# A norm's mean from chunk sums on POOL or DVE and one matmul with ones, in a Mamba and feed-forward layer on one Trainium2 core

## The chip, the core and the metric

The kernel runs on one core of a Trainium2 chip. The metric is the device time of one execution in microseconds (us); lower is better. The engines are named as in the profile: PE (TensorE, matmuls), PEld (its weight loads), DVE (VectorE), ACT (ScalarE), POOL (GpSimd) and SP (SyncE, which here issues nearly all DMAs). All data are fp32.

## The reference

The input x has 8 sequences of 384 channels and 32 x 32 = 1,024 positions. What is computed, cut to what matters:

```python
def ln(v, eps):                       # over the 384 channels of a position
    m = v.mean(channels); s = v.var(channels)
    return (v - m) / sqrt(s + eps)

# for each sequence
t  = ln(ln(x, 1e-6), 1e-5) * ln_w + ln_b
xm, z = split(t @ in_proj.T)          # 768 + 768
xc = silu(conv3(xm) + conv_b)         # causal, along the positions
dt, Bm, Cm = split(xc @ x_proj.T)     # 24, 16, 16
dt = softplus(dt @ dt_proj.T + dt_b)  # 768
h  = exp(dt * A) * h + dt * xc * Bm   # recurrence along positions: 768 x 16 states
y  = ((h * Cm).sum(states) + xc * D) * silu(z)
t  = gelu((y @ out_proj.T) @ w1.T + b1) @ w2.T + b2
x  = x + t
# for the first 5 sequences: binarised weights, absmax quantisation per sequence
t  = quant(gelu(quant(ln(x, 1e-5) @ W1b.T + b1)) @ W2b.T + b2)
x  = x + t                            # sequences 5 to 7: quant returns zeros, so x stays
```

## The kernel before

**Tiles.** Channels lie on the 128 partitions in KC = 3 chunks, positions along the free axis in two halves of T = 512 columns. A tile of 384 channels and one half is [128, 3, 512]. Weights come in 128 x 128 blocks as the stationary operand.

**Stages.** `s1` makes the two norms (as one, with a joint eps), the input projection (p_in, p_z), the convolution, dt, B and C for each half of a sequence and stores them in HBM. `s2` with `scan` and `scan_pair` is the recurrence: 12 units to a sequence, in each four groups of four states; per group POOL multiplies by B (line 968), ACT makes the exponentials (line 577, tile da, in PSUM), DVE scans (line 993), POOL or DVE multiplies by C, and PE sums the states of two groups with eight matmuls of 32 columns (line 933, py). The first and the last sequence are scanned in two halves, the others whole. `s3` is the output projection and the MLP (p_out, p_h, p_o). `ffn` is the feed-forward part of the first five sequences (p_y). `binarise` prepares its weights once.

**The norm.** `norm` (line 610) is called 26 times: 16 times from `s1`, 10 times from `ffn`. For the mean, `columns` sums over the channels with matmuls against ones. There are twelve of them (line 619, p_sum), each 128 x 32 against 128 columns. Three accumulate for each of four column groups, which lie in the four 32-partition strips of the array. The result is scaled by -1/384 on ACT or DVE (tile mean), and `spread` (line 637, p_mean) brings it to all partitions by four matmuls with a broadcast column of the identity. DVE adds it to the three chunks (line 649). The variance goes the same way: ACT squares (tile sq), twelve matmuls (p_var), a scaling, a small matmul that turns it (line 659), an add, a power on POOL (line 665), `spread` again (p_r) and a multiplication on DVE (line 669).

**The order.** Nothing is left to a scheduler at run time. `Plan` is a planner in the kernel's own code: each operation is added with an engine, a cost in us, what it reads and writes, and perhaps a second engine with another cost (`others`). `Plan.run` walks through time in a model, takes for each engine the operation that `choose` and `rank` prefer among those that are ready, and emits it; so each engine's queue gets its order. Costs are constants and small functions (MM for a whole 128x512 matmul, `c_act`, `c_dve`, `c_pair`, `c_pool`), `LAG` is what an engine may overlap, SIGNAL and DRAIN what a hand-over costs, `land` and `size` stand for a DMA. TURNS holds a number for each 100 us of the model's time; it turns the order of operations of equal rank and has bits that let scans or stages go first. On DVE and POOL an operation outside the scan is preferred to the scan's own unless a bit says otherwise. Where the model sees PE idle for more than IDLE = 0.7 us, it emits small matmuls that nobody reads (line 471, spare) so that PE goes on working.

**Rings.** Every tile is taken from a ring of a fixed number of buffers (lines 428 to 445), and an operation that needs a new tile waits for a free one. The rings named below are front (7 buffers, results of `s1`), w_f (3, its weights), dt_r (3, dt for the scan), sq (1, squares and the product dt * xc) and mm (3, PSUM for matmuls).

Of the kernel before, what the change touches and what calls it, by code (L numbers as in the profile page):

```python
# [70 lines left out]

MM = 0.86
SWITCH = 0.22
# [18 lines left out]
TURNS = (  # L92
    17610, 24087, 20212, 39788, 55575, 59023, 81989, 22321, 58617, 812894,
    311620, 51673, 560357, 59520, 80314, 2104, 50573, 559844, 6159, 58063,
    51278, 41401, 6390, 863060, 0, 672911, 34250, 39179, 27191, 131575,
)
# [7 lines left out]

LAG = {"ACT": 0.09, "DVE": 0.08}

# [9 lines left out]
def c_pair(n):  # L116
    return 0.22 + n * 0.00188

# [78 lines left out]
class Op:  # L197
    __slots__ = (
        "engine", "cost", "emit", "prio", "slack", "table", "size",
        "wants", "next", "ready", "tiles", "others", "settle", "land",  # L200
    )


class Plan:
# [12 lines left out]
    def add(self, engine, cost, emit, r=(), w=(), claim=(), table=None, size=0, others=None,  # L217
            land=1.6, rate=350e3):
        op = Op()
        op.engine, op.cost, op.emit, op.table = engine, cost, emit, table  # L220
        op.others, op.settle = others or {}, None
        op.size, op.land, op.prio = 0.03 + size / rate, land + 0.2, (*self.prio, len(self.ops))
        op.next, op.ready, op.tiles = [], 0.0, []
        op.slack = SLACK if self.prio[0] < 0 else 0.0
        deps = set()

        def parts_of(t):
            t, part = t if isinstance(t, tuple) else (t, None)
            if t not in op.tiles:
                op.tiles.append(t)  # L230
                if t.ring is not None:
                    t.left += 1
            if part is None:
                if None not in t.parts:
                    t.parts[None] = [None, []]
                return list(t.parts.values())
            if part not in t.parts:
                whole = t.parts.get(None)
                t.parts[part] = [whole[0], list(whole[1])] if whole else [None, []]
            return [t.parts[part]]  # L240

        for t in claim:
            t.left += 1
            op.tiles.append(t)
        for t in r:
            for p in parts_of(t):
                if p[0] is not None:
                    deps.add(p[0])
                p[1].append(op)
        for t in w:  # L250
            for p in parts_of(t):
                if p[0] is not None:
                    deps.add(p[0])
                deps.update(p[1])
                p[0], p[1] = op, []
        deps.discard(op)
        op.wants = len(deps)
        for d in deps:
            d.next.append(op)
        self.ops.append(op)  # L260
        return op

    def run(self):
# [5 lines left out]
        free["PE"] = 2 * SIGNAL  # L269
        table, dma_free, clock = None, 0.0, Clock()  # L270
        left, scanned = len(self.ops), 0
# [17 lines left out]
        def choose(e, now, able):  # L289
            able = [op for s, op in able if s <= now]  # L290
            at = int(now / STRETCH)
            turn = TURNS[at] if at < len(TURNS) else 0
            if e == "ACT":
                same = [op for op in able if op.table == table and table != "exp"]
                plain = [op for op in able if op.table in (None, "exp")]
                able = same if table is not None and same else plain or able
                if turn & ACT_STAGES:
                    able = [op for op in able if op.prio[0] > 0 and op.table in (None, "exp")] or able
                if len(self.spare.ring.free) <= SCARCE:
                    able = [op for op in able if self.spare.ring in map(ring_of, op.tiles) and (  # L300
                        op.table in (None, "exp", table))] or able
            if e in ("DVE", "POOL"):

                scans = [op for op in able if op.prio[0] == 0]
                if not (turn & (DVE_SCANS if e == "DVE" else POOL_SCANS) and scans):
                    able = [op for op in able if (
                        op.prio[0] > 0 and op.ready <= now - PATIENCE)] or scans or able
                else:
                    able = scans
            return min(able, key=lambda op: rank(op, turn))  # L310
# [29 lines left out]
        while left:  # L340
# [28 lines left out]
            if e == "PE":  # L369
                while now - free[e] > IDLE and self.spare.ring.free[0:] and (  # L370
# [7 lines left out]
                    free[e] = clock.run(free[e], MM / 2)  # L378
                    heapq.heappush(ring.free, free[e])
            for t in taken_by(op):  # L380
                heapq.heappop(t.ring.free)
                t.ring.taken[t.lane] += 1
                t.real = t.ring.make(t.shape, t.name)
            op.emit()
            cost = op.cost
            if op.table is not None and op.table != table:
                cost += LOAD_TABLE
                table = op.table
            end = clock.run(now, cost) if e == "PE" else now + cost
            free[e] = end - LAG.get(e, 0.0)  # L390
            if e == "SP":
# [19 lines left out]
class Layer:  # L411
    def __init__(self, ctx, tc, a, out):
# [9 lines left out]
        def ring(tag, bufs, where=sbuf):  # L422
# [6 lines left out]

            "front": ring("front", 7), "t_f": ring("t_f", 2), "w_f": ring("w_f", 3),  # L430
            "dbc": ring("dbc", 1), "halo": ring("halo", 2),

            "dt_r": ring("dt_r", 3), "dtx_r": ring("dtx_r", 2), "u": ring("u", 3),
            "xr": ring("xr", 1), "zr": ring("zr", 1), "state": ring("state", 1),
# [7 lines left out]

            "mm": ring("mm", 3, psum), "sq": ring("sq", 1),
            "rstd": ring("rstd", 2), "root": ring("root", 2),
# [127 lines left out]

    def act(self, out, in_, func, cost, r, w, table=None, **kw):

# [4 lines left out]
            }),  # L579
            r=r, w=w, table=table,  # L580
        )

    def affine(self, out, in_, r, w, bias=0.0, scale=1.0, n=T, pool=False):
# [21 lines left out]
        else:  # L605
            others = {"DVE": (c_dve(n) + (0 if isinstance(scale, float) else 0.15), on(nc.vector))}
        extra = 0.0 if plain else 0.09 if isinstance(scale, float) else 0.18
        self.plan.add("ACT", 0.16 + n * 0.00083 + extra, on_act, r=r, w=w, others=others)

    def norm(self, t, eps, scale):  # L610

        nc, add = self.nc, self.plan.add
        def columns(src, name):
# [10 lines left out]

            add("PE", 0.78, emit, r=[src], w=[p])
            return p

        def spread(src, name, turned=False):
# [12 lines left out]

            add("PE", 0.98, emit, r=[src], w=[p])
            return p

        p_sum = columns(t, "p_sum")
        mean = self.piece("rstd", [P, TG], "mean")
        self.affine(lambda: mean.real, lambda: p_sum.real, [p_sum], [mean], scale=-1.0 / C, n=TG)
        p_mean = spread(mean, "p_mean")
        add("DVE", c_dve(KC * T), lambda: nc.vector.tensor_add(
            t.real, t.real, p_mean.real.unsqueeze(1).to_broadcast([P, KC, T])  # L650
        ), r=[p_mean], w=[t])
# [6 lines left out]
        p_turned = self.piece("mm", [P, G], "p_turned")  # L658
        add("PE", 0.3, lambda: nc.tensor.matmul(
            p_turned.real, var.real, self.ident[:, ::DQ], start=True, stop=True  # L660
        ), r=[var], w=[p_turned])
        rstd = self.piece("root", [P, G], "rstd")
        add("DVE", 0.1, lambda: nc.vector.tensor_scalar_add(rstd.real, p_turned.real, eps),
            r=[p_turned], w=[rstd])
# [10 lines left out]
    def s1(self, b):  # L675
# [45 lines left out]
        for half, cols in enumerate(HALVES):  # L721
# [58 lines left out]

            add("PE", 0.15 + KC * MM, low, r=[w, *all_m], w=[p_dbc], claim=[dbc])
            self.affine(lambda dbc=dbc: dbc.real, lambda p_dbc=p_dbc: p_dbc.real, [p_dbc], [dbc])
# [12 lines left out]
            for k in range(0, KD, 2):  # L795
# [14 lines left out]

                add("PE", MM + 0.2, two, r=[dbc, *dict.fromkeys(ws)], w=pds, claim=[dt.pieces[k // PER]])
                for i in range(2):
# [39 lines left out]
    def scan(self, b, half, state):  # L852
# [21 lines left out]
        for m in range(KC * per_p):  # L874
# [12 lines left out]
            def unit(name, p=p):  # L887
# [7 lines left out]
            xr = unit("xc")  # L895
            self.act(lambda py=py: py.real, lambda xr=xr: xr.real, AF.Identity, c_act(T),
                     r=[xr], w=[py], scale=skip[:, m : m + 1])
# [18 lines left out]
            for q in range(NQUAD):  # L916
# [21 lines left out]
                with self.plan.lane(-1):  # L938
                    add("PE", SWITCH + BATCH * MM, sums, r=[u for _, u in batch], w=[py])
                batch = []  # L940
# [19 lines left out]
    def scan_pair(self, u, cols, n, dts, dtxs, bq, cq, state, half, on_pool):  # L960
# [14 lines left out]
        for t, mine in enumerate(cols):  # L975
            da = self.piece("da", [P, wide, n], "da")
            dt_r = dts[t]
            for i, col in enumerate(mine):
                self.act(
                    lambda i=i, da=da: da.real[:, i, :],  # L980
                    lambda i=i, dt_r=dt_r: dt_r.real[:, i, :], AF.Exp,
                    0.25 + n * 0.00084, r=[dt_r[i]], w=[da], table="exp",
                    scale=self.a_neg[:, col : col + 1],
# [130 lines left out]
    def binarise(self, name, kt, n_out):  # L1114
# [25 lines left out]
        for ks, ms in pieces:  # L1140
# [11 lines left out]

            add("PE", 0.25 + MM, total, r=[w], w=[pm])
            if ks.stop == kt:
# [10 lines left out]
        p_mean = self.piece("mm", [P, NUM_GROUPS, 2], "p_means")  # L1165
        add("PE", 0.3, lambda: nc.tensor.matmul(
            p_mean.real, self.ones[:rows, :], sums.real[:rows], start=True, stop=True
# [29 lines left out]
    def quant_scale(self, mx, n):  # L1197
# [11 lines left out]

        add("PE", 0.25, lambda: nc.tensor.matmul(  # L1210
            p_max.real, self.ones, diag.real, start=True, stop=True
# [196 lines left out]
```

## Time and profile before

The three times are 3152.11, 3156.54 and 3156.19 us, with a median of 3156.19 us. The profile is of a fourth execution.

| | |
|---|---|
| profiled execution | 3154.12 us |
| its span | 3152.0 us |
| granted clock of PE, mean | 0.992 |
| DMA, share of 16 engines | 71.2%, 239 GB/s |
| records on PE | 10962 |
| p_sum, records and busy | 624, 22.6 us |
| p_mean, records and busy | 208, 29.3 us |
| spare, records and busy | 218, 58.9 us |
| table loads on ACT | 194, 248.9 us |

A matmul of the code is two records on PE. Busy time is given from the first start to a modelled end and includes the pipeline's tail; two records in a row overlap, so the cost of one is read from start to start. In a line of groups the numbers after the bar are busy time, mean ns of one record, and the idle time in front with what ended it.

### The profile page before, as it was taken

The page shows a single profiled execution, that of the slowest core. Times are in us where ns is not written, and L with a number is a line of the kernel's source. Part 1 is how long each engine was busy: PE and PEld are TensorE (multiplying, and loading weights), DVE is VectorE, ACT ScalarE, POOL GpSimd, SP SyncE. Part 2 cuts the span into 40 slices and gives each one's busy share as a digit, 9 for nine tenths or more (in the row PEclk, how much of TensorE's full clock was granted, in tenths as well). Part 3 has the DMA queues.
Part 4 walks back from the last instruction along what each step waited for, and adds up shares of the span by engine and source line. Part 5 has one row for each costly group of instructions (what it writes and reads, how often), then busy time and mean ns, then how long its engine had stood idle before and what let it go on. Part 6 is the DMA issues. An engine that isn't in the chain of part 4 may idle for free.

```text
span 3152.0 us, 33796 instructions
## 1 busy us (share of the span) xinstructions
PE 3073.8 (98%) x10962; PEld 1274.0 (40%) x10962; DVE 2602.0 (83%) x2056; ACT 2000.8 (63%) x2409; POOL 2747.2 (87%) x1047
## 2 busy tenths in 40 slices
PE   9989999999999999999999999999999999999999
PEld 4334334444443344433444343434434443333334
DVE  3787888889888899888899788997888988887881
ACT  4889787667557466665665676666665565655661
POOL 1788888998999988999989999989998999988990
PEclk9999999999999999999999999999999999999999
DMA  6889878867678668766686786876777857756542
GB/s 223 301 308 302 268 246 295 274 221 269 228 269 291 212 204 284 273 230 208 207 321 221 241 275 207 283 239 227 250 236 242 277 189 232 229 175 189 171 149 73
DMA packets 348974, 751.85 MB, mean 239 GB/s; under 512 B 36480, under 2 KB 113792, under 8 KB 339584
## 3 DMA queue, kind: packets, MB, share of 16 engines
q1 hardware_dynamic: 348368, 749.61, 71.2%
q8 instruction: 88, 1.44, 0.2%
q14 instruction: 86, 0.70, 0.1%
q10 hardware_dynamic: 432, 0.09, 0.0%
HBM read 569.21 MB, written 180.36 MB: 238 GB/s over the span
## 4 chain that ended last, share of the span: by engine, by line
PE 72%; DVE 7%; DMA 7%; ACT 6%; POOL 5%; issue 3%; SPq 1%; DVEq 0%; POOLq 0%; ACTq 0%
PE p_y L561 15%; PE p_o L561 14%; PE p_h L561 14%; PE py L933 9%; PE p_out L561 6%; PE p_in L561 5%; PE p_z L561 5%; POOL u L968 3%; DVE u L993 2%; DVE da L993 2%; ACT da L577 2%; DMA dtx_r<-dtx_d 1%; ACT L577 1%; PE p_dt L806 1%; DMA w<-in_out_proj_w 1%
## 5 line engine op out<-in xcount | busy, mean ns | idle before, releaser
L968 POOL TENSOR_TENSOR u<-dtx_r,bc 128x2048 f32<-128x2048 f32 (+1 forms) x360 | 1186.7, 3312 | 91.8 <-PE py L933 48.9
L577 ACT ACTIVATE da<-dt_r,a_neg 128x1024 f32<-128x1024 f32 (+1 forms) x960 | 898.8, 945 | 547.9 <-DVE u L993 307.2
L968 POOL TENSOR_TENSOR u<-u,bc 128x2048 f32<-128x2048 f32 (+1 forms) x274 | 901.1, 3292 | 122.3 <-DVE u L993 96.1
L993 DVE TENSOR_TENSOR_SCAN u<-da,u 128x1024 f32<-128x1024 f32 (+1 forms) x436 | 871.1, 2009 | 147.6 <-POOL u L968 78.7
L561 PE MATMUL p_h<-t,w_b 128*128 128x512 f32 x1152 | 518.3, 603 | 11.5 <-DMA w_b<-in_mlp_w 6.9
L561 PE MATMUL p_o<-g,w 128*128 128x512 f32 x1152 | 510.2, 596 | 4.7 <-DMA w<-in_mlp_w 3.3
L993 DVE TENSOR_TENSOR_SCAN da<-da,dtx_r 128x1024 f32<-128x1024 f32 (+1 forms) x192 | 381.9, 2015 | 37.2 <-POOL dtx_r L968 23.7
L968 POOL TENSOR_TENSOR dtx_r<-dtx_r,bc 128x2048 f32<-128x2048 f32 (+1 forms) x120 | 397.0, 3312 | 4.0
L561 PEld LDWEIGHTS p_h<-t,w_b 128*128 128x128 f32 x1152 | 216.1, 192 | 301.0 <-issue 255.3
L561 PEld LDWEIGHTS p_o<-g,w 128*128 128x128 f32 x1152 | 214.8, 190 | 290.8 <-issue 273.2
L561 PE MATMUL p_y<-gf,w_n 128*128 128x512 f32 x720 | 321.4, 600 | 3.9 <-DVE t L669 2.6
L561 PE MATMUL p_y<-tn,w_b 128*128 128x512 f32 x720 | 319.3, 597 | 5.7 <-DVE tn L669 2.6
L933 PE MATMUL py<-u,fold 128*32 128x512 f32 x2304 | 302.5, 626 | 0.0
L993 DVE TENSOR_TENSOR_SCAN da<-da,u 128x1024 f32<-128x1024 f32 (+1 forms) x140 | 282.9, 2041 | 19.6 <-ACT da L577 9.2
L577 ACT ACT_TABLE_LOAD x194 | 248.9, 1283 | 3.5
L561 PE MATMUL p_out<-yg,w 128*128 128x512 f32 x552 | 245.0, 595 | 3.3 <-DMA w<-in_out_proj_w 2.5
L561 PE MATMUL p_z<-t,w_f 128*128 128x512 f32 x504 | 227.6, 598 | 8.9 <-DMA w_f<-in_in_proj_w 4.7
L561 PE MATMUL p_in<-t,w_f 128*128 128x512 f32 x504 | 229.2, 601 | 3.5 <-issue 2.3
L561 PEld LDWEIGHTS p_y<-gf,w_n 128*128 128x128 f32 x720 | 134.5, 191 | 189.6 <-issue 171.1
L561 PEld LDWEIGHTS p_y<-tn,w_b 128*128 128x128 f32 x720 | 133.9, 190 | 184.8 <-issue 162.3
L592 ACT ACTIVATE g<-p_h,v_vecs 128x512 f32<-128x512 f32 x160 | 109.1, 682 | 118.1 <-PE p_h L561 117.8
L592 ACT ACTIVATE y<-p_y,v_vecs 128x512 f32<-128x512 f32 x139 | 94.8, 682 | 126.4 <-PE p_y L561 95.0
(132 smaller groups left out, 3228.9 us busy)
## 6 DMA issues: line engine op xcount, KB each, us to landing
dt_r<-dt_d SPq DMA_DIRECT2D x144, 512.0 KB, 5.1
dtx_r<-dtx_d SPq DMA_DIRECT2D x72, 1024.0 KB, 6.0
w_b<-in_mlp_w SPq DMA_DIRECT2D x192, 192.0 KB, 3.2
w<-in_mlp_w SPq DMA_DIRECT2D x96, 384.0 KB, 3.5
w_f<-in_in_proj_w SPq DMA_DIRECT2D x168, 192.0 KB, 3.9
y_d<-y SPq DMA_DIRECT2D x120, 256.0 KB, 5.2
gf<-y_d SPq DMA_DIRECT2D x60, 512.0 KB, 6.8
xc_d<-xc SPq DMA_DIRECT2D x48, 512.0 KB, 6.7
```

The costliest lines, as they stand in the source:

```text
L561: self.nc.tensor.matmul(p.real, w.real[:, w0 + k, :], t.at(k0 + k), start=start and k == 0, stop=stop and k == n - 1,)
L577: lambda: self.nc.scalar.activation(out(), in_(), func, **{k: v() if callable(v) else v for k, v in kw.items()}),
L592: nc.scalar.activation(out(), in_(), AF.Identity, bias=bias, scale=scale)
L806: nc.tensor.matmul(pds[i].real, ws[i].real[rows, (k + i) % KC, :], dbc.real[rows, :], start=True, stop=True,)
L933: nc.tensor.matmul(py.real[g * DQ : (g + 1) * DQ, :], self.fold, hc, start=False, stop=(q == NQUAD - 1), skip_group_check=True,)
L968: nc.gpsimd.tensor_mul(u.real[:, x], t.real[:, x], row.real.unsqueeze(2).to_broadcast([P, n, 2]))
L993: da=da, in_u=in_u: nc.vector.tensor_tensor_scan(to(i), da.real[:, i, :], in_u(i), state.real[:, col : col + 1] if half else 0.0, ALU.mult ...
```

## The change

The mean of a norm is made in another way. The three chunks are added element by element into a tile total [128, 512], by two adds on POOL or by one reduction on DVE, as the planner chooses. One matmul with a 128 x 128 matrix of ones then gives the sum over channels on all partitions, and the scale -1/384 moves into the subtraction. The variance is made as before.

The planner counts a cost MODE when PE goes from a tiled matmul to a whole one or back, and prefers a tiled operation after a tiled one. A filler counts as whole. Tiled are p_var, p_dbc, p_dt, py and the sums of `binarise`. Several costs, the lag of POOL and the time a DMA needs to land are set anew. The rings front, w_f, dt_r and sq change size, and TURNS has new numbers.

```diff
-MM = 0.86
+MM = 0.859
+MODE = 0.097
...
-LAG = {"ACT": 0.09, "DVE": 0.08}
+LAG = {"ACT": 0.09, "DVE": 0.08, "POOL": 0.045}
...
 def c_pair(n):
-    return 0.22 + n * 0.00188
+    return 0.19 + n * 0.001905
...
-        op.size, op.land, op.prio = 0.03 + size / rate, land + 0.2, (*self.prio, len(self.ops))
+        op.size, op.land, op.prio = 0.03 + size / rate, land - 0.1, (*self.prio, len(self.ops))
...
+            if e == "PE" and tiled:
+                able = [op for op in able if op.tiled] or able
...
+            if e == "PE" and op.tiled != tiled:
+                cost, tiled = cost + MODE, op.tiled
             end = clock.run(now, cost) if e == "PE" else now + cost
-            free[e] = end - LAG.get(e, 0.0)
+            free[e] = end - (LAG.get(e, 0.0) if guest else op.lag)
...
-            "front": ring("front", 7), "t_f": ring("t_f", 2), "w_f": ring("w_f", 3),
+            "front": ring("front", 6), "t_f": ring("t_f", 2), "w_f": ring("w_f", 4),
-            "dt_r": ring("dt_r", 3), "dtx_r": ring("dtx_r", 2), "u": ring("u", 3),
+            "dt_r": ring("dt_r", 2), "dtx_r": ring("dtx_r", 2), "u": ring("u", 3),
-            "mm": ring("mm", 3, psum), "sq": ring("sq", 1),
+            "mm": ring("mm", 3, psum), "sq": ring("sq", 2),
...
-        p_sum = columns(t, "p_sum")
-        mean = self.piece("rstd", [P, TG], "mean")
-        self.affine(lambda: mean.real, lambda: p_sum.real, [p_sum], [mean], scale=-1.0 / C, n=TG)
-        p_mean = spread(mean, "p_mean")
-        add("DVE", c_dve(KC * T), lambda: nc.vector.tensor_add(
-            t.real, t.real, p_mean.real.unsqueeze(1).to_broadcast([P, KC, T])
+        total = self.piece("sq", [P, T], "total")
+
+        def in_two():
+            nc.gpsimd.tensor_add(total.real, t.real[:, 0, :], t.real[:, 1, :])
+            nc.gpsimd.tensor_add(total.real, total.real, t.real[:, 2, :])
+
+        def at_once():
+            nc.vector.tensor_reduce(
+                total.real, t.real.rearrange("p k l -> p l k"), AX.X, ALU.add
+            )
+
+        add("POOL", 2.5, in_two, r=[t], w=[total], others={
+            "DVE": (c_dve(KC * T) + 0.02, at_once)
+        })
+        p_mean = self.piece("mm", [P, T], "p_mean")
+        add("PE", MM, lambda: nc.tensor.matmul(
+            p_mean.real, self.ones, total.real, start=True, stop=True
+        ), r=[total], w=[p_mean])
+        add("DVE", c_dve(KC * T) + 0.05, lambda: nc.vector.scalar_tensor_tensor(
+            t.real, p_mean.real.unsqueeze(1).to_broadcast([P, KC, T]), -1.0 / C, t.real,
+            ALU.mult, ALU.add,
         ), r=[p_mean], w=[t])
```

Left out are the numbers of TURNS and the other costs that are set anew (for example 0.98 to 0.89 for `spread`, 0.3 to 0.14 for the small turning matmul). They change no instruction by themselves, but can change its place.

## The prediction

> **What bounds the kernel.** I read the page's head first, then the slices, then the waits of TensorE, then the time lines of single instructions.
>
> ```profile
> span 3152.0 us, 33796 instructions
> ...
> PE 3073.8 (98%) x10962; PEld 1274.0 (40%) x10962; DVE 2602.0 (83%) x2056; ACT 2000.8 (63%) x2409; POOL 2747.2 (87%) x1047
> ...
> PE   9989999999999999999999999999999999999999
> ...
> POOL 1788888998999988999989999989998999988990
> ```
>
> PE is busy from end to end, so the end is set by what PE has to do plus what it waits. A busy PE includes pipeline tails, so I made the sum again from start to start. One line of the code is two records (the page counts 2304+768 py records for 192 sums of eight products), and a full 128x512 record takes 0.429 us when nothing interferes. 5,472 such records (p_h, p_o, p_y, p_out, p_in, p_z) are 2,348 us; 192 sums py at 1.94 are 372; 48 pairs p_dt at 1.06 are 51; 16 p_dbc at 2.73 are 44; the 26 norms at about 3.5 are 91; the rest is about 24; 518 changes between tiled and whole matmuls (below) at 0.099 are 51. That is 2,981 us of work. The 109 fillers (L471) at 0.436 are 48, which do nothing but bridge planned gaps. The remaining 123 us are waits, about half of them in the first 500 us. PE is therefore the bound, and POOL, at 87%, is the nearest other.
>
> **What one norm costs on PE, and a change of mode.** This stretch of PE's time line has all of it; the columns are start, length with the pipeline's tail, and how many records.
>
> ```profile
> 2009.86 0.83 PE L619 MATMUL p_sum<-tn,small 128*32 128x128 f32 x24
> 2010.63 2.84 PE L561 MATMUL p_y<-tn,w_b 128*128 128x512 f32 x6
> 2013.31 1.05 PE L637 MATMUL p_mean<-mean,ident 128*128 128x128 f32 x8
> 2014.20 4.03 PE L561 MATMUL p_z<-t,w_f 128*128 128x512 f32 x9
> ```
>
> From start to start: p_sum 0.77 us (0.79 where a whole matmul stands in front), p_mean 0.89. The six p_y between them take 2.68, where six records elsewhere take 6 x 0.429 = 2.57: 0.10 us more because a tiled matmul (32 columns) went before. A whole matmul in front of a tiled one pays the same, as here, where 18 records take 7.82 = 7.72 + 0.10 ahead of py, and the four behind it 1.82 = 1.72 + 0.10:
>
> ```profile
> 1336.84 7.89 PE L561 MATMUL p_in<-t,w_f 128*128 128x512 f32 x18
> 1344.66 2.00 PE L933 MATMUL py<-u,fold 128*32 128x512 f32 x16
> 1346.62 1.98 PE L561 MATMUL p_y<-gf,w_n 128*128 128x512 f32 x4
> 1348.44 1.88 PE L561 MATMUL p_out<-yg,w 128*128 128x512 f32 x4
> ```
>
> **The change part by part.**
>
> PE's work. Gone: 26 x 0.79 = 20.5 us (p_sum) and 26 x 0.89 = 23.1 (p_mean). New: 26 whole matmuls 128x512 at 2 x 0.429 = 0.86, 22.3 us. Net -21.3 us.
>
> Changes of mode. Counted in the two instruction orders, from tiled (p_sum, p_var, p_dbc, p_dt, py, p_sums) to whole or back: 518 before, 458 after. 16 of the p_sum stood alone between whole matmuls, which is 32 of the 60; the others come from the new preference for a tiled operation after a tiled one. 60 x 0.099 = -5.9 us. A preferred tiled op can hold up a whole matmul that another engine waits for, by at most one op (2.7 us, p_dbc); PE's own sum does not change by it, so I price that at nothing.
>
> Fillers. 109 before, 119 after: +10 x 0.436 = +4.4 us. They also tell where gaps are planned: during the first sequence's scans 38 before and 69 after, in the next five 19 and 5, in the last two with what follows 52 and 45. The price of the early gaps is in these numbers.
>
> Waits that go. PE waits at p_mean for the scaled sums:
>
> ```profile
> PE p_mean L637 <- DVE mean L599: 2.1, 3, 0.9
> ...
> PE p_mean L637 <- ACT mean L592: 1.9, 3, 0.7
> ```
>
> These 4.0 us (the first number after each colon) go with the hop over ACT or DVE. The wait of p_sum for x's load, 2.3 us in the same view, stays, at p_mean. In their place p_mean can wait for POOL: between 0 and 26 x 2.6 = 67 us if PE had nothing else. In the orders other matmuls stand between except at the start, so I take 0 beyond the start. There (7.39 to 8.74 in the trace, first p_sum to first p_mean, 1.35 us) two adds take 2.56 us and a hop: +1.3 us, with fillers under it.
>
> The adds. The norm's sum is made 23 times on POOL and 3 times on DVE in the new order. The rows near it:
>
> ```profile
> L1305 POOL TENSOR_TENSOR x<-x,y 128x512 f32<-128x512 f32 x30 | 37.8, 1281 | 1.2 <-DMA w_b<-in_mlp_w 0.6 <-POOL u L968 0.3
> ...
> L949 DVE TENSOR_TENSOR zr<-py,zr 128x512 f32<-128x512 f32 x84 | 56.7, 675 | 25.8 <-PE py L933 25.6
> ...
> L649 DVE TENSOR_TENSOR t<-t,p_mean 128x1536 f32<-128x1536 f32 x16 | 27.9, 1745 | 6.5 <-PE p_mean L637 6.5
> ```
>
> POOL: 23 x 2 x 1.281 = 59 us more, 2,806 in all. DVE: 3 reductions over 1,536 elements at 1.75 (row L649) are 5 us; the subtraction as a three-operand instruction is 0.06 to 0.17 us longer (such an instruction of 512 elements, L741 and L1082, takes 0.738 against 0.675), 2 to 4 us; 5 scalings go. ACT: 21 scalings at 0.27 go (-5.6), but the new order has 214 table loads for 195, 19 x 1.283 = +24. ACT comes to about 2,020 of 3,130, 65%: PE's work covers it; uncovered it would cost the 24.
>
> **Here a rule speaks against the change.** The Trainium skill, GPSIMD Engine Reference, Engine selection, sends elementwise adds to VectorE because GpSimd is about half as fast with two inputs. The rows agree on the ratio (1.281 to 0.675). By the rule the adds belong on DVE: 26 x 2 x 0.675 = 35 us there, 0 on POOL, and the 59 us on the second busiest engine are a loss. By the trace it matters only where POOL ends last:
>
> ```profile
> 900.00:2700.00 1800.00, 1687.31 (x509) 0.99 0.72 244
> ```
>
> In the middle POOL (second number) works 1,687 of 1,800 us. 12 of the 26 norms lie there: 12 x 2.56 = 31, and with a stretch shortened by 16 us POOL would be at 1,718 of 1,784, 96%. It still fits, so I take 0. The second objection is in SBUF — State Buffer, SBUF: two separate sides: GpSimd and a DVE instruction with two SBUF inputs lock each other out for a whole instruction. By that, up to 59 us of DVE could be blocked. The rows say otherwise: the 324 scans of 128x1024 beside this busy POOL take 2.285 us in the mean and the longest of any scan is 2.31; one operand of DVE's large instructions lies in PSUM, as p_mean does. 0 again.
>
> Rings. dt_r 3 to 2: the load for the next unit is issued when the last exponential of the old one ends. Around 1,430 us such a last one ends at 1,431.7 and the next unit's first starts at 1,440.5; the page gives 5.1 us from issue to landing. It fits by 3.7 us; for the unit's second tile (1,436.5 to 1,441.6) by nothing. Between 0 and 96 x 2 us = 192 if every unit slipped by 2; 0 taken, since the scans also queue on POOL's products. front 7 to 6 lets a store be waited for; w_f 4 and sq 2 loosen waits (w_f 4.7 us at p_z, sq 2.2 at p_var). Together 0, between -7 and +10. The number of DMAs on SP's queue is unchanged (2,253 instructions both times). The ties and the corrected costs reorder all engines; the total work stays, so they can only act on the 123 us of waits: from -45 to +25, and I take 0, having no row for it.
>
> **Sum.** -21.3 - 5.9 + 4.4 - 4.0 + 1.3 = -25.5. From the profiled execution, 3,154.1 us (span 3,152.0 and 2.1 around it), that gives 3,128.6. The median of the three times shown is 2.1 above that execution and the lowest 2.0 below, so I leave it: **3,128 us**.
>
> **Rivals.**
> 1. *The order follows the hardware better* (chance 0.24). The plan did not price the 518 changes (51 us) and now does; it counts landings earlier. For it: half of the waits lie in the first 500 us and few are planned gaps. If a quarter of the 123 us goes: 3,128 - 31 = 3,097. Against: more fillers are planned early.
> 2. *The gain is swallowed* (0.10). PE gives up 27 us, but in the middle the scans set the pace, and PE waits at py instead. For it: POOL at 95 to 99% in many slices. Against: PE's matmuls show no wait for POOL's products at all, only weight loads do (18.9 us). Time: 3,154, give or take 5.
> 3. *POOL becomes the bound* (0.06, slower). One mechanism: the two adds go in front of the scan's products, since norm work is chosen ahead of scans, and each holds POOL by 2.56 us; it decides from the point at which POOL's idle time in the middle, now 113 us, is no longer where the adds fall. Of the 59 us some 46 fall after the first 500 us; paid half, without PE's gain showing: 3,154 + 23 = 3,177. For it: idle POOL waits mostly for DVE's scans and for py, so it is a loop and idle time cannot be moved at will. Against: the new order has fewer fillers there (5 for 19).
> 4. *The mode is not saved* (0.05): the 0.10 us belongs to the 32-column weights and comes back in p_var's place. Then +5.9: 3,134, inside the forecast's own range.
>
> The forecast itself has 0.55, with an own range of 3,108 to 3,142 (its costs between the ends given, without the extreme ones). **Range** for 8 in 10: 3,092 to 3,151, which takes in most of rival 1 and a part of rival 2. A difference under 0.2% (6 us) can't be told from none; faster than that needs less than 3,149.9. Chances: faster 0.87 (forecast, 1, 4 and a quarter of 2), within 0.06 (most of the rest of 2), slower 0.07 (3 and an end of 2).
>
> **What would show it.** Right: no p_sum; p_mean 26 x 2 records at 0.43 from start to start; a PE of 27 us less work; POOL near 2,806 with 46 new instructions of 1.28; PE still 98%. Wrong: a wait of PE for POOL's sums or for exponentials behind dt_r; POOL over 97% in the middle; gaps ahead of py; a first py much later than now (109 us in).

## The result, and the profile after

The changed kernel takes 3,132.75 us (median of four runs, 3,131.12 to 3,135.08) against 3,156.04 us before (the three times above and a fourth of 3,155.89). The ratio is 0.9931, with a 95% interval of 0.9916 to 0.9946. That is 23 us or 0.7% faster. The forecast was 3,128 us.

The page of the kernel after, its head and the slices of PE and POOL:

```profile
span 3130.3 us, 32297 instructions
...
PE 3049.4 (97%) x10202; PEld 1243.8 (40%) x10202; DVE 2599.5 (83%) x2053; ACT 2019.1 (65%) x2406; POOL 2802.1 (90%) x1095
...
PE   9899999999999999999999999999999999999999
...
POOL 2889888999999998999989998999999999999880
```

PE has 760 records fewer and is still busy from end to end. POOL went from 2,747 to 2,802 us. The time line of PE shows the new matmul after a tiled sum, and the price of the change of mode:

```profile
2416.69 1.11 PE L956 MATMUL py<-u,fold 128*32 128x512 f32 x8
2417.62 1.08 PE L956 MATMUL py<-dtx_r,fold 128*32 128x512 f32 x8
2418.63 1.12 PE L667 MATMUL p_mean<-total,small 128*128 128x512 f32 x2
2419.59 5.31 PE L568 MATMUL p_out<-yg,w 128*128 128x512 f32 x12
2424.83 0.43 PE L626 MATMUL p_var<-sq,small 128*32 128x128 f32 x8
```

From start to start p_mean takes 0.96 us here, which is 0.86 and 0.10 for the tiled py in front of it. Twelve records of p_out take 5.24, which is 5.15 and 0.09 for the tiled p_var behind them.

Made again in the same way, PE's sum is as follows.

| us | before | after |
|---|---|---|
| work of PE, start to start, with changes of mode | 2,977 | 2,950 |
| fillers | 50 | 53 |
| waits | 121 | 122 |
| behind the last matmul | 4 | 4 |
| span | 3,152 | 3,130 |

The work differs by 27 us, the fillers by 4 (49.7 and 53.3) and the waits by 1. By stretches the waits did move: in the first 500 us 60 and then 58, from there to 2,700 us 41 and then 54, behind that 20 and then 10. The fillers in the first 500 us went from 17 to 31 us. The adds, the reductions and the subtraction, from the views by tile of the kernel after:

```profile
L655 POOL TENSOR_TENSOR total<-t x14: 1261/1282/1304, 5.6 to 1634.1; 128x512 f32<-128x512 f32 x14
...
L659 DVE TENSOR_REDUCE total<-t x2: 1902/1907/1912, 445.8 to 903.9; 128x512 f32<-128x1536 f32 x2
...
L670 DVE SCALAR_TENSOR_TENSOR t<-p_mean,t x16: 1730/1745/1759, 10.1 to 2010.6; 128x1536 f32<-128x1536 f32 x16
```

An add takes 1.28 us, as the row of before said (the three numbers are least, median and most in ns). And these are waits of PE, first of before, then of after (sum, times, longest):

```profile
PE p_r L637 <- POOL rstd L665: 1.8, 2, 1.3
```

```profile
PE p_r L644 <- POOL rstd L687: 7.5, 3, 3.8
...
PE p_mean L667 <- POOL total L656: 2.7, 2, 2.1
```

The 4.0 us that PE waited for the scaled mean are gone. In their place are 2.7 for the sum and 5.7 more for the power. The power stands in the same queue of POOL as the adds, but it is not the adds that make it late: in no_adds below, which has none, PE still waits 7.0 us for it.

```profile
PE p_r L644 <- POOL rstd L684: 7.0, 3, 3.5
```

The longer wait comes with the new order.

### The profile page after: what moved, and what is told of

It is laid out like the page before. It is cut to its first block, busy times and chain, and to the rows that moved or that the text cites. A ratio compares the mean times of both kernels' runs of the same rounds, so it can differ in the third digit from the quotient of the medians.

```text
span 3130.3 us, 32297 instructions
## 1 busy us (share of the span) xinstructions
PE 3049.4 (97%) x10202; PEld 1243.8 (40%) x10202; DVE 2599.5 (83%) x2053; ACT 2019.1 (65%) x2406; POOL 2802.1 (90%) x1095
## 4 chain that ended last, share of the span: by engine, by line
PE 53%; DVE 6%; DMA 5%; ACT 5%; POOL 4%; issue 2%; SPq 0%; DVEq 0%; POOLq 0%; ACTq 0%
PE p_y L568 16%; PE p_o L568 11%; PE p_h L568 9%; PE py L956 7%; PE p_out L568 5%; POOL u L992 3%; DVE u L1017 2%; PE p_in L568 2%; DVE da L1017 2%; PE p_z L568 2%; ACT da L584 1%; ACT L584 1%; DMA w_b<-in_mlp_w 1%; DMA w<-in_mlp_w 1%; DMA w_n<-bin_w 1%
## 5 line engine op out<-in xcount | busy, mean ns | idle before, releaser
L1037 DVE TENSOR_TENSOR dtx_r<-da,bc 128x1024 f32<-128x1024 f32 x144 | 170.8, 1214 | 0.1
```

The costliest lines, as they stand in the source:

```text
L1037: nc.vector.tensor_mul(u.real[:, 0, :, t], da.real[:, 0, :], cq.real)
```

## The experiments

In the table, "PE's sum" is PE's work, changes of mode and fillers by the kernel's instruction order, at the durations of the trace of before. The kernels were measured in four groups, in which the kernel before had medians of 3,156.0, 3,156.9, 3,158.7 and 3,159.8 us. The ratio is to the one of the same group, so a few us between two rows of the table mean nothing.

| kernel | changes of mode | fillers | PE's sum | median, us | median less sum | ratio to before (95%) |
|---|---|---|---|---|---|---|
| before | 518 | 109 | 3,026 | 3,156.0 | 130 | 1 |
| after | 458 | 119 | 3,003 | 3,132.8 | 130 | 0.9916 to 0.9946 |
| mean_twice | 458 | 119 | 3,025 | 3,146.3 | 121 | 0.9952 to 0.9974 |
| adds_twice | 458 | 119 | 3,003 | 3,178.8 | 176 | 1.0046 to 1.0087 |
| no_adds | 458 | 119 | 3,003 | 3,131.7 | 129 | 0.9899 to 0.9943 |
| no_fill | 454 | 0 | 2,950 | 3,142.5 | 192 | 0.9934 to 0.9980 |
| before_no_ties | 540 | 172 | 3,055 | 3,248.7 | 194 | 1.0267 to 1.0309 |
| norm_without_ties | 520 | 222 | 3,054 | 3,243.4 | 190 | 1.0253 to 1.0288 |
| old_norm_without_ties | 488 | 141 | 3,037 | 3,227.6 | 191 | 1.0202 to 1.0237 |
| after_no_ties | 472 | 161 | 3,022 | 3,200.5 | 178 | 1.0113 to 1.0161 |
| no_mode_count | 502 | 265 | 3,071 | 3,235.5 | 165 | 1.0225 to 1.0256 |
| old_rings | 464 | 182 | 3,031 | 3,233.8 | 203 | 1.0212 to 1.0246 |
| sums_on_dve | 470 | 164 | 3,023 | 3,225.8 | 202 | 1.0190 to 1.0220 |
| after_with_old_ties | 474 | 338 | 3,100 | 3,286.1 | 186 | 1.0376 to 1.0413 |

### Four with the order held fast

These four keep the changed kernel's order on every engine and alter only what an operation issues; the planner isn't told.

**mean_twice**

```diff
+        def summed():
+            for _ in range(2):
+                nc.tensor.matmul(p_mean.real, self.ones, total.real, start=True, stop=True)
+
-        add("PE", MM, lambda: nc.tensor.matmul(
-            p_mean.real, self.ones, total.real, start=True, stop=True
-        ), r=[total], w=[p_mean])
+        add("PE", MM, summed, r=[total], w=[p_mean])
```

> The matmul with ones is issued twice in each of the 26 norms, in the same place of the order of every engine; the result is the same. PE has 26 x 0.858 = 22.3 us more work and no other engine has any. If PE's own work sets the end (the prediction), the time rises by about 22 us, from 3,133 to 3,150 to 3,160. If the scan's engines or the loads set the pace and PE has slack (gain swallowed), the second matmul falls into waits: under 8 us more, 3,133 to 3,141.

The median rose by 13.5 us, and the profiled execution, at a span of 3,149.6, by 19.3. The single runs spread from 3,136 to 3,153. The median lies between the two expectations, the profiled execution (3,151.4 us) in the first. In the profiled execution the sum of work and fillers rose by 22 and the waits fell by 3. So most of an added microsecond on PE comes through: 61% by the medians and 87% by the profiled executions. The rival under which PE's saving falls into waits would have it below 8 and is out.

**adds_twice**

```diff
         def in_two():
+            nc.gpsimd.tensor_add(total.real, t.real[:, 0, :], t.real[:, 1, :])
+            nc.gpsimd.tensor_add(total.real, total.real, t.real[:, 2, :])
             nc.gpsimd.tensor_add(total.real, t.real[:, 0, :], t.real[:, 1, :])
             nc.gpsimd.tensor_add(total.real, total.real, t.real[:, 2, :])
```

> The two adds on POOL are each issued twice, in the same order otherwise; the sum is the same. POOL has 23 x 2 x 1.28 = 59 us more, 2,861 of about 3,140 us. If POOL's work is covered by PE (the prediction): at most 8 us more, up to 3,141. If POOL is near to being the bound: 30 to 59 us more, 3,163 to 3,192.

**no_adds**

```diff
         def in_two():
-            nc.gpsimd.tensor_add(total.real, t.real[:, 0, :], t.real[:, 1, :])
-            nc.gpsimd.tensor_add(total.real, total.real, t.real[:, 2, :])
+            pass
...
-            nc.vector.tensor_reduce(
-                total.real, t.real.rearrange("p k l -> p l k"), AX.X, ALU.add
-            )
+            pass
...
-            p_mean.real, self.ones, total.real, start=True, stop=True
+            p_mean.real, self.ones, t.real[:, 0, :], start=True, stop=True
```

> The sums over the chunks are left out, on POOL and on DVE; the matmul with ones reads the first chunk alone, so the mean is that of a third of the channels. The order is otherwise the same. POOL has 59 us less, DVE 6 less. If POOL's adds are covered (the prediction): within 5 us of 3,133, apart from some 1.3 us at the start. If the adds hold up the scans: 15 to 45 us faster, 3,088 to 3,118.

These two experiments belong together. Without any add the time is 1 us lower, well inside the intervals: the adds, as the change has them, cost nothing that can be measured. Issued a second time, the same adds cost 46 us of their 59. PE's waits in adds_twice:

```profile
PE p_mean L670 <- POOL total L659: 19.0, 9, 5.4
PE p_h L568 <- DMA w_b<-in_mlp_w: 12.4, 9, 2.3
PE p_r L644 <- POOL rstd L690: 10.2, 4, 3.7
```

and its page:

```profile
PE 3066.4 (96%) x10202; PEld 1249.4 (39%) x10202; DVE 2602.5 (82%) x2053; ACT 2018.5 (64%) x2406; POOL 2861.8 (90%) x1141
```

The share of POOL is 90% as in the changed kernel, so it is not a POOL without gaps. PE comes to p_mean nine times before the sum is there (19 us, where the changed kernel has 2.7). But for two, PE's records stand in the same order in both traces, so its delay can be followed from record to record. Of 48 us, 20 arise at p_mean, 5 at p_r behind the power and 11 at p_h, where PE waits for weights; the rest is spread over many lines. 18 us are lost in the first 500 us, where POOL is busy for 394 of 500, and 12 in the next 400. The order had been laid out for sums that are ready 2.6 us earlier, and PE takes its matmuls in the order of its queue. So half of the loss is lateness at fixed places of PE's queue. That the other half follows from the same lateness, and not from the amount of POOL's work, is likely but not shown.

**no_fill**

```diff
                     self.spare.real = ring.make(self.spare.shape, self.spare.name)
-                    self.fill()
+                    pass
```

> The 119 fillers are not issued; all else stands in the same order. If they stand in gaps that PE has anyway (the prediction took them so), the time stays within 6 us of 3,133, or rises by up to 15 where PE's granted clock falls in a gap. If PE runs behind the plan, so that the gaps have closed by the time PE comes to them, fillers are work for nothing: up to 119 x 0.436 = 52 us faster, 3,081 to 3,115.

The time rose by 10 us and the mean granted clock fell from 0.993 to 0.986. Of 53 us of fillers taken out, 63 came back as waits:

```profile
PE p_r L644 <- POOL rstd L687: 12.2, 5, 3.5
...
PE p_mean L667 <- POOL total L656: 7.6, 3, 5.4
...
PE py L956 <- POOL u L992: 5.7, 2, 3.4
```

So the gaps under the fillers of the changed kernel are real, and there a change in the number of fillers may be counted as a change in gaps, as the prediction did.

### Eight with the order made anew

Here the planner sees the edit, and every engine's order changes. A table of ties was found for one list of operations. So that no kernel has to run with the table of another, seven of them run without any (`TURNS = ()`).

**before_no_ties and after_no_ties**

```diff
-TURNS = (
-    59965, 29935, 54697, 25830, 41556, 52704, 5806, 54013, 24204, 552223,
...
-)
+TURNS = ()
```

> The kernel before with an empty table of ties, so that operations of equal rank go in the order written. Its instruction order holds 540 changes of mode, 172 fillers and 3,055 us of PE work, fillers among it, at the durations of the trace. Both measured kernels lie about 129 us above that sum (waits, tail, what lies around the span). If the sum by the order decides: 3,184, within 10. If fillers beyond the old number only stand where PE would wait anyway, or waits vary freely between orders: anywhere from 3,150 to 3,215, apart from the sum.

> The changed kernel with an empty table of ties: 472 changes of mode, 161 fillers, 3,022 us by its order. With the 129 us above: 3,151, within 10. Beside the kernel before without ties it tells what the norm, the planner's costs and the rings bring without a table: 33 us by the sums. If the table of ties is what made the kernel faster, the two without a table are within 10 us of each other.

Both are far slower than expected, by 65 and 50 us. Fillers and changes of mode were in these expectations, so the miss is waits: some 180 us in each trace instead of 121. The medians differ by 48 us, twice what the two kernels with their tables show. But the runs of after_no_ties spread from 3,196 to 3,210 us, and its profiled execution is the slowest of the four, while that of before_no_ties is the fastest of its four. These two differ by 33 us, all of it in PE's sum. So 33 us are work and fillers, and whether the waits differ too, by 15 us, is open. By the medians a table is worth 93 us in the kernel before and 68 in the changed one.

**after_with_old_ties** is the changed kernel with the 30 numbers of before.

```diff
 TURNS = (
-    59965, 29935, 54697, 25830, 41556, 52704, 5806, 54013, 24204, 552223,
+    17610, 24087, 20212, 39788, 55575, 59023, 81989, 22321, 58617, 812894,
...
```

> The changed kernel with the table of ties of the kernel before. Its order holds 338 fillers, 474 changes of mode and 3,100 us by its sum, 77 over the changed kernel without ties, which took 3,200. If a table is worth something only for the list of operations it was found for: 3,230 to 3,290, slower than without any. If a table helps by itself (its bits let stages go first at certain times): 3,140 to 3,195.

It takes 3,286 us, 86 slower than with no table at all. This table helps only with the list of operations it was found for; its numbers turn the order of operations by their place in the list, and each new norm has one operation fewer.

**norm_without_ties** puts the norm of the changed kernel, as printed in the diff above, into the kernel before, without a table. **old_norm_without_ties** puts the old one into the changed kernel; its edit is this one turned round.

```diff
-        p_sum = columns(t, "p_sum")
...
+        total = self.piece("sq", [P, T], "total")
...
```

> The new norm alone in the kernel before, no ties in either: old costs, old rings, no count of changes of mode. 520 changes, 222 fillers, 3,054 us by its order: 23 us less work than the kernel before without ties and 22 us more fillers. If the planned gaps are real: 3,183, as the kernel before without ties. If the norm's saving comes through by itself whatever the plan: 3,155 to 3,165.

> The changed kernel with the old norm put back, no ties in either: 488 changes, 141 fillers, 3,037 us by its order, 14 us over the changed kernel without ties. By the sum: 3,166, within 10, 14 slower than that. If the new norm's gain is swallowed by POOL: no slower than the changed kernel without ties, 3,140 to 3,152.

With the old costs and rings the norm brings 5 us, and the intervals overlap: nothing that can be told. Its 23 us of PE work turned into 22 us of fillers. The new tile total also takes a buffer of the ring sq, which has one buffer in this kernel: POOL stands idle for 7.5 us until p_var gives it free. With the new costs and rings the same norm brings 27 us by the medians. Of these, 14 are in PE's sum. The other 13 are less sure, since the two profiled executions differ by 18 us only.

**no_mode_count, old_rings, sums_on_dve**, all without a table:

```diff
-MODE = 0.097
+MODE = 0.0
...
-            if e == "PE" and tiled:
-                able = [op for op in able if op.tiled] or able
```

> The changed kernel without the count of changes of mode and without the preference for a tiled operation after a tiled one, no ties. 502 changes for 472, which is 3 us of PE work; 265 fillers for 161, 45 us. If the count of modes acts by keeping the plan beside PE's real pace: 25 to 60 over the 3,200 of the changed kernel without ties. If it acts by the changes saved alone: 3 us over it, 3,195 to 3,210.

```diff
-            "front": ring("front", 6), "t_f": ring("t_f", 2), "w_f": ring("w_f", 4),
+            "front": ring("front", 7), "t_f": ring("t_f", 2), "w_f": ring("w_f", 3),
-            "dt_r": ring("dt_r", 2), "dtx_r": ring("dtx_r", 2), "u": ring("u", 3),
+            "dt_r": ring("dt_r", 3), "dtx_r": ring("dtx_r", 2), "u": ring("u", 3),
-            "mm": ring("mm", 3, psum), "sq": ring("sq", 2),
+            "mm": ring("mm", 3, psum), "sq": ring("sq", 1),
```

> The changed kernel with the four rings of before (front 7, w_f 3, dt_r 3, sq 1), no ties. 3,031 us by its sum, 8 over the changed kernel without ties. If the rings do nothing much (the prediction took 0, between 7 faster and 10 slower for the change): 3,193 to 3,212. If the loads behind two dt_r held up the scans: faster than without, under 3,190. If the longer rings were what helped: over 3,215.

```diff
-        add("POOL", 2.5, in_two, r=[t], w=[total], others={
-            "DVE": (c_dve(KC * T) + 0.02, at_once)
-        })
+        add("DVE", c_dve(KC * T) + 0.18, at_once, r=[t], w=[total])
```

> The sum over the chunks as one reduction on DVE in all 26 norms, no ties. POOL has 59 us less, DVE 23 x 1.91 = 44 more; the sum by the order is 3,023, as without ties. If neither engine decides: 3,193 to 3,210. If POOL is the one that is short: 15 us or more faster than the 3,200 with POOL's adds, under 3,186. If DVE is short: over 3,215.

Beside the 3,200.5 us of after_no_ties these are 35, 33 and 25 us slower. The run without the count of modes is in the range of the first theory: 104 fillers (45 us) more and only 3 us of changes of mode. It leaves out the count and the preference at once, so it does not tell which of the two did it. The rings come out against the expectation of nothing: 9 of their 33 us are in PE's sum. Where sq has one buffer, PE waits longer at p_var for the squares; these lines are of old_rings and of after_no_ties:

```profile
PE p_var L622 <- ACT sq L580: 9.9, 3, 5.0
```

```profile
PE p_var L622 <- ACT sq L580: 5.8, 4, 2.9
```

Over all seven orders without a table this wait is 9.9, 12.7 and 15.1 us where sq has one buffer, and 2.4, 3.2, 5.8 and 6.2 where it has two. Loads of w_f show the same less cleanly (5.7, 10.2 and 12.1 with three buffers; from nothing to 9.5 with four). The 4 us at p_var are a small part of what the rings bring; where the rest arises is not shown. Nothing speaks for a loss through two buffers of dt_r. The pages of after_no_ties and of sums_on_dve show where the sums went:

```profile
PE 3089.7 (96%) x10286; PEld 1264.3 (39%) x10286; DVE 2602.7 (81%) x2058; ACT 2020.9 (63%) x2397; POOL 2803.9 (87%) x1097
```

```profile
PE 3102.5 (96%) x10292; PEld 1272.5 (39%) x10292; DVE 2646.7 (82%) x2089; ACT 2040.8 (63%) x2407; POOL 2747.6 (85%) x1051
```

POOL is 56 us lighter than in after_no_ties, DVE 44 heavier, and the kernel 25 us slower. Had POOL been short of time, it should have been faster. But this is one order of each kernel.

One caution holds for these eight. Undoing the norm, the count of modes and the rings one at a time costs 27, 35 and 33 us, 95 together; undoing all three, with the other costs, costs 48. So the single losses don't add up (the norm's tile total, for one, draws on the ring sq), and each kernel is one order among many. How much of each 25 to 35 us is the part that was undone, and how much is after_no_ties having a lucky order, is not settled: it would take several orders of each kernel.

## Why the prediction was right, point by point

**PE's work.** Forecast: 21.3 us less through the norm, 5.9 through modes. In the trace PE's work fell by 27. The price of a whole matmul (0.858) and of a change of mode (0.10) hold at the new place. mean_twice says that PE's work does set the end, at 61 to 87% of its size. One detail of the working is wrong: by its own list of tiled operations 11 of the p_sum, not 16, stood alone between whole matmuls, which is 22 of the 60 changes; five more stand behind p_dbc, which is tiled. The count of 60 holds.

**Fillers as gaps.** Forecast +4.4 us; they are +4, and no_fill shows them to stand for real gaps. This term had to be counted in the new order. norm_without_ties shows why: there the same saving of PE's work is used up by 22 us of fillers. So the 23 us belong to the norm together with the order that was found for it, and no run here has the norm's own share in the kernels with tables.

**Waits.** Forecast: 4.0 us of waits for the scaled mean less, 1.3 more at the start. The first is gone, but waits for POOL's power and sum came to 8.4 us more, and the first product p_in starts at 23.7 us, not 21.8. This term was mis-sized: -2.7 in the sum, +1 in the trace, and it is the difference between 3,128.6 and the profiled 3,132.1. The power's part of it is due to the order and not to the adds (no_adds). One sign of being wrong came in a small way: the first py starts at 116.7 us instead of 109.2. It was made up for, as the waits behind 2,700 us fell from 20 to 10.

**POOL.** The adds are 58.6 us by their rows, and hidden (no_adds, -1 us). POOL was to be at 96% in the middle. The same stretch after the change, in which POOL is the last of the busy times, shows it:

```profile
900.00:2700.00 1800.00, 1775.70 (x5912) 720.30 (x5911) 1564.78 (x1114) 1126.71 (x1214) 1710.89 (x535) 1.00 0.73 244
```

1,711 of 1,800 is 95%. But the cover was thinner than "it still fits" says: the next 59 us in the same places cost 46. Rival 3 had its price nearly right, for twice the adds, and its point of decision wrong: 30 of the 48 us are lost in the first 900 us, before the stretch in which it saw POOL run full, and 20 of the 48 arise where a sum comes later than its place in PE's queue.

**The rule against adds on POOL.** The Trainium skill, GPSIMD Engine Reference, Engine selection, would have sent the sums to DVE. The ratio it gives is in the rows, the reduction on DVE took 1.91 us against 2.56 for two adds, and yet the one order with all sums on DVE was 25 us slower. As no_adds shows POOL's adds to be free, there was nothing to gain. That DVE scans lengthen beside POOL's adds is not seen: the 324 scans of 128x1024 are at 2.285 us (the second number behind the bar, in ns) before and after:

```profile
L993 DVE TENSOR_TENSOR_SCAN u<-da,u 128x1024 f32<-128x1024 f32 x324 | 739.5, 2285 | 109.9 <-POOL u L968 66.6 <-ACT da L577 30.9 <-POOL dtx L821 1.1
```

```profile
L1017 DVE TENSOR_TENSOR_SCAN u<-da,u 128x1024 f32<-128x1024 f32 x324 | 739.5, 2285 | 116.8 <-POOL u L992 56.9 <-ACT da L584 48.1
```

Each of them reads one operand from PSUM, though, so they can't tell what a DVE instruction with two inputs in SBUF would have suffered.

**The ties and the costs, taken at 0.** Here the forecast had no row to go by. It took the waits as unchanged, and they are (121 and 122 us), but that was in part luck. The term holds two results of a search: the old table won 93 us, the new one 68, so 25 less. On the other side, without tables the rest of the change (norm, costs, rings) is worth 48 us by the medians, not 25, so 23 more than the forecast's sum. About 8 of the 23 are PE's work and fillers of these other orders and 15 lie outside PE's sum; the two traces show no such difference in waits (181 and 180). Whether the waits stay by themselves or two terms balance is therefore open. The range given for the term, from -45 to +25, holds either, the second only just. Of the rivals, the first (the order follows the hardware better) has something for it without tables: norm_without_ties to after_no_ties is 43 us, of which 32 are in PE's sum, mostly 61 fillers fewer. In the kernels as they stand it doesn't show.

**The mode is not saved** (rival 4) is out, though the 3,134 us that it named came nearer to the measured time than the forecast: p_mean pays 0.10 us only beside a tiled neighbour, and the sum of work fell by the full 27.

## What to carry to other kernels

In a kernel whose order is fixed ahead, sum up the bounding engine's work and idle fillers from the instruction order with durations from start to start; that gave this change to within some 4 us. Then distrust the part called waits: it stayed at 121 us here, but was some 180 in the same kernels without their tables, and the old table in the changed kernel was worse than none. Before moving work to a second engine because it has slack, double it in place: what is free once cost four fifths of its length the second time, at a share of busy time that was 90% both times. Ask when each result is due in the bounding engine's queue, and not only how busy the second engine is.

## What the runs showed of the hardware that was not expected

A subtraction with three operands over 1,536 elements, one of them in PSUM and broadcast, takes 1.745 us on DVE, exactly as the plain add did; 0.06 to 0.17 more had been estimated from shorter instructions. A reduction of 1,536 elements to 512, which reads them in a turned order, takes 1.91 us, 0.16 more than a pass over as many elements in order; 1.75 had been taken for it. And taking out work that nobody reads (the fillers) made the kernel 10 us slower, with the mean granted clock of PE 0.007 lower.
